# A pre-norm transformer block in float32: ScalarE's round-trip instructions queued behind the latest copy out of PSUM, and another spread of steps in the values' sweep

## The chip, the cores and the metric

The kernel runs on one core of one Trainium2 chip. A core has five engines that work side by side, each through its own queue in order: TensorE (PE in the profile; its weight loads are PEld), VectorE (DVE), ScalarE (ACT), GpSimd (POOL) and SyncE (SP, which here only issues DMAs). PE writes its products to PSUM, a small memory of its own; ACT and DVE copy from there to SBUF, the working memory. The metric is device time in microseconds (us) of the whole program, lower is better.

## The reference, cut to what matters

Input is one sequence of 2048 positions by 1024 features, everything float32. The feed-forward part has three weights of 2752 x 1024, which are put through a "round trip" before they are used: each block of 64 consecutive weights is divided by its largest absolute value, each quotient is replaced by the nearest of 16 fixed codes (NF4), and the block is multiplied by the same value again.

```python
def block(x):                                   # x: 2048 x 1024
    n = layernorm(x)
    q, k, v = (n @ w.T + b for w, b in ((wq, bq), (wk, bk), (wv, bv)))
    # 32 heads of 32; heads attend to heads within one position
    probs = softmax(einsum("shd,std->sht", q, k) / sqrt(32))
    x = x + einsum("sht,std->shd", probs, v)
    n = layernorm(x)
    w1, w2, w3 = (round_trip(w) for w in (W1, W2, W3))
    return x + (silu(n @ w1.T) * (n @ w2.T)) @ w3.T
```

## The kernel before, in words

**Products.** Large products are done with seven block products in place of eight (Strassen's scheme in Winograd's form). Operands are split in halves both ways, sums and differences of the quarters are made on DVE, and PE makes seven products 1 to 7. Some of them accumulate onto one another in PSUM: `z` takes products 1, 6, 5 and 3 in turn, and between two of them ACT has to copy the present state of `z` out (g0, u2, u4). So the next product into `z` waits for that copy. These are the copies that PE waits for.

**Stages.** First come three sweeps over eight pairs of 128-position tiles: queries, keys, values (`products`, line 348, called from the three loops at 531, 623 and 713). Within `products`, a function `fill(n)` is called behind each product; it puts other PE work between the products: transposes of the next tile (`transposes`, 467, or `keep_T`, 688), parts of the scores or of the context (`part`, 604; many small 32 x 32 products), and steps of the background. Then the feed-forward part ("the feed-forward stage" here) runs over 22 chunks of the hidden dimension: class `Unit` (877) makes the gate and up products and their Silu, and `down7` (980) the product with w3, whose results `give` (1000) copies to SBUF (`acc`, six buffers) and adds to x1 in DRAM by an accumulating DMA from POOL.

**The background: the round trip.** All 65 chunks of w1, w2 and w3 ("jobs") go through a generator, `background` (219), that is advanced a step at a time from the other code. A job is a load `wn` (SP); the largest values of the blocks (DVE, line 207); a division (16 ACT instructions of 64 columns, `scaled`, 192, line 195); 15 steps over 1024 columns, of which 12 are a pair, an ACT instruction that writes `sg` (line 242, two buffers) and a DVE instruction that merges it into `r` (line 243), and 3 are DVE alone (234, 236, 238); and the multiplication by the block's value, in the sweeps by 16 ACT instructions (line 195 again), in the feed-forward stage in turn by those or by one DVE instruction (line 254). Then `finish` (147) follows: PE transposes `r` in two halves of four (`ptw`, line 161), ACT copies each half out (`wop`, line 162), DVE makes the sums, SP stores the result, and a later DMA loads it as a weight.

**What sets the order.** PE's queue is in the order in which the program is traced (`manual_schedule` for PE, line 283): every transpose of `finish` has a fixed place between the products. The queues of ACT, DVE, POOL and SP are ordered when the kernel is built, by a planner that follows the dependences and its own idea of when each instruction can start; among instructions that it thinks ready, the one that was traced earlier goes first. An instruction of the background may so be put ahead of work that was traced long before it. In the sweeps the background advances by the numbers in `fill` (725 to 735 in the values' sweep, where `advance(2 if n == 6 else 1)` makes seven steps a pair of tiles) and by `advance(2)` after each pair; in the feed-forward stage by time: `spent` (794) advances 0.69 steps per microsecond of product. `pending` holds the jobs that wait for `finish`; `flush` (187) runs some of it, in the feed-forward stage mostly when the next job has reached its sixth step, or at once where a weight is needed (`until`, 264).

Of the kernel before, what the change touches and what calls it, by code (L numbers as in the profile page):

```python
# [2 lines left out]

# [1 line left out]

# [64 lines left out]
def preln_block_kernel(  # L70
# [38 lines left out]
    dqp = ctx.enter_context(tc.tile_pool(name="dq", bufs=2))  # L109
    fs = ctx.enter_context(tc.tile_pool(name="fs", bufs=2))  # L110
    hook = {"scale": "ACT"}

    def mean_var(pool, src, dst):
        st = pool.tile([P, 2, 6], FP, tag="st", name="st")
# [76 lines left out]

    def scaled(dst, src, by, nb):

        for n in range(nb):
            nc.scalar.mul(dst[:, ts(n, BLOCK)], src[:, ts(n, BLOCK)], by[:, n : n + 1])  # L195

    def width(kind, c):
        return KC * min(P, F - c * P) if kind == "3" else E
# [20 lines left out]
    def background():  # L219
        ready = load_w(*jobs[0])  # L220
        ahead = load_w(*jobs[1])
        am = absmax(*jobs[0], ready)
        yield
        for n, (kind, c) in enumerate(jobs):
            wn, wa = ready, am
            ready = ahead
            if n + 2 < len(jobs):
                ahead = load_w(*jobs[n + 2])
            w = width(kind, c)
            v = wn[:, :w]  # L230
            r = dqp.tile([P, E], FP, tag="r", name="r", bufs=2)[:, :w]
            for i, (side, edge, code) in enumerate(STEPS):
                if i == 0:
                    nc.vector.tensor_scalar(r, v, edge, code, ALU.is_lt, ALU.mult)
                elif side == "<":
                    nc.vector.scalar_tensor_tensor(r, v, edge, r, ALU.is_lt, ALU.max)
                elif side == ">":
                    nc.vector.scalar_tensor_tensor(r, v, edge, r, ALU.is_gt, ALU.subtract)
                else:
                    t = dqp.tile([P, E], FP, tag="sg", name="sg")[:, :w]  # L240
                    by = BIG if side == "+" else -BIG
                    nc.scalar.activation(t, v, AF.Copy, bias=-edge * by, scale=by)  # L242
                    nc.vector.scalar_tensor_tensor(r, t, code, r, ALU.min, ALU.max)  # L243
                step["n"] = i
                yield
                if i == 9 and n + 1 < len(jobs):
                    am = absmax(*jobs[n + 1], ready)
                    yield
            if hook["scale"] == "ACT" or n % 2:
                scaled(r, r, wa, w // BLOCK)  # L250
            else:
                r3 = r.rearrange("p (b e) -> p b e", e=BLOCK)
                f = wa[:, : w // BLOCK].unsqueeze(2).to_broadcast([P, w // BLOCK, BLOCK])
                nc.vector.tensor_tensor(r3, r3, f, ALU.mult)
            pending.append(finish(kind, c, r))
            yield
# [91 lines left out]
    def products(A, fill, used=lambda name: None, apart=None):  # L348

        def mul(dst, a, w, start, stop):
            mm4(dst, A[:, a], W[w], start, stop)
            used(w)

        def copied(nm, src):
            t = pair.tile([P, TB], FP, tag=nm, name=nm)
            nc.scalar.copy(t, src)  # L358
            return t

        z = ps_pj.tile([P, TB], FP, tag="z", name="z")
        mul(z, SA11, "B11", True, False)
        g0 = copied("g0", z)
        q = ps_pj.tile([P, TB], FP, tag="q", name="q")
        mul(q, S3, "T3", True, False)
        s7 = copied("s7", q)
        fill(7)
        mul(z, S2, "T2", False, False)
        u2 = copied("u2", z)
        fill(6)  # L370
        r = bank("r")
        mul(r, SA12, "B21", True, True)
        ce = pair.tile([P, E], FP, tag="C0", name="ce")
        co = pair.tile([P, E], FP, tag="C1", name="co")
        nc.vector.tensor_tensor(ce[:, 0:512], g0, r, ALU.add)
        fill(2)
        mul(z, S1, "T1", False, apart is not None)
        u4 = copied("u4", z)
        nc.vector.tensor_tensor(co[:, 512:], u4, s7, ALU.add)
        fill(5)  # L380
        if apart is None:
            mul(z, S4, "B22", False, True)
            nc.scalar.copy(ce[:, 512:], z)
        else:
            y = apart.tile([P, TB], FP, tag="y", name="y", bufs=1)
            mul(y, S4, "B22", True, True)
            nc.vector.tensor_tensor(ce[:, 512:], u4, y, ALU.add)
        fill(3)
        mul(q, SA22, "T4", False, True)
        nc.vector.tensor_tensor(co[:, 0:512], u2, q, ALU.add)  # L390
        fill(4)
        return ce, co
# [62 lines left out]
    class Inputs:  # L455
# [11 lines left out]
        def transposes(self, j):  # L467
            for half in range(2):
                pt = ps_t.tile([P, 4, P], FP, tag="pt", name="pt")
                for k in range(4):  # L470
                    nc.tensor.transpose(pt[:, k, :], self.xn[j][:, ts(4 * half + k, P)], ident)
                n = (SA11, SA12, SA21, SA22)[2 * j + half]
                a, v = (self.a21, self.v21) if n == SA21 else (self.A[:, n], self.V[:, n])
                nc.scalar.copy(a, pt)
                nc.scalar.copy(
                    v.rearrange("p k (c m) -> p k c m", c=4),
                    pt.rearrange("p k (m c) -> p k c m", c=4),
                )

        def finished(self):  # L480
# [207 lines left out]
    def keep_T(i, x1n):  # L688

        t = work.tile([P, 2, 4, P], FP, tag=f"xT{i % 2}", name="xT")  # L690
        for half in range(2):
            pt = bank("pt").rearrange("p (k t) -> p k t", t=P)
            for k in range(4):
                nc.tensor.transpose(pt[:, k, :], x1n[:, ts(4 * half + k, P)], ident)
            nc.scalar.copy(t[:, half], pt)
        cols = ts(i // 2 % 4, P)
        tbp = i // 8
        names = ("B11", "B21") if i % 2 == 0 else ("B12", "B22")
        for n in range(2):
            nc.sync.dma_start(xd[names[n], tbp][:, :, cols], t[:, n])  # L700
        if i % 2 == 0:
            even["t"] = t
            return
        b11, b21 = even["t"][:, 0], even["t"][:, 1]
        b12, b22 = t[:, 0], t[:, 1]
        u = {}
        for n in range(4):
            u[n + 1] = work.tile([P, 4, P], FP, tag="xU", name="xU", bufs=2)
            y, z = ((b12, b11), (b22, u.get(1)), (b22, b12), (b21, u.get(2)))[n]
            nc.vector.tensor_tensor(u[n + 1], y, z, ALU.subtract)  # L710
            nc.sync.dma_start(xd[f"T{n + 1}", tbp][:, :, cols], u[n + 1])

    for p in range(NP):
# [9 lines left out]
        def fill(n):  # L723
            if n in (7, 2, 5, 4) and (p, n) != (1, 7):
                part()
            advance(2 if n == 6 else 1)
            if n in (7, 4):
                flush(1)
            if n == 5 and i in x1n:
                keep_T(i, x1n.pop(i))  # L730
            if n == 3:
                if p == 0:
                    part()
                elif i + 1 in x1n:
                    keep_T(i + 1, x1n.pop(i + 1))
# [141 lines left out]
    class Unit:  # L877
# [13 lines left out]
        def first(self):  # L891
            self.z = ps_z.tile([P, TB], FP, tag="z", name="z")
            self.mul(1, self.z, True, False)
            self.g0 = hp.tile([P, TB], FP, tag="g0", name="g0", bufs=2)
            nc.scalar.copy(self.g0, self.z)

        def middle(self):
            q = self.q = ps_q.tile([P, TB], FP, tag="q", name="q")
            self.mul(7, q, True, False)
            self.mul(6, self.z, False, False)  # L900
            u2 = self.u2 = hp.tile([P, TB], FP, tag="u2", name="u2")
            nc.scalar.copy(u2, self.z)  # L902
            r = ps_r.tile([P, TB], FP, tag="r", name="rr")
            self.mul(2, r, True, True)
            nc.vector.tensor_tensor(self.g0, self.g0, r, ALU.add)
            nc.scalar.activation(self.g0, self.g0, AF.Silu)
            self.mul(5, self.z, False, False)
            u4 = hp.tile([P, TB], FP, tag="u4", name="u4")
            nc.scalar.copy(u4, self.z)  # L909
            self.h = [new_h(), new_h()]  # L910
            nc.vector.tensor_tensor(self.h[1], u4, q, ALU.add)

        def last(self, odd_done=None):
            self.mul(3, self.z, False, True)
            si = hp.tile([P, TB], FP, tag="si", name="si")
            nc.scalar.activation(si, self.z, AF.Silu)
            nc.vector.tensor_tensor(self.h[1], self.h[1], si, ALU.mult)
            if odd_done:
                odd_done(self.h[1])
# [60 lines left out]
    def down7(g, tbp, sides):  # L980
# [18 lines left out]

        def give(src, q, *places):  # L1000
            t = accp.tile([P, TB], FP, tag="acc", name="acc")
            nc.scalar.copy(t, src)  # L1002
            for j, n in places:
                nc.gpsimd.dma_start(x1d[8 * tbp + 2 * q + j][n], t, accum_op=ALU.add)  # L1004

# [161 lines left out]
```

## Time and profile before

| What | Value |
|---|---|
| Median of 3 runs (lowest, highest) | 2488.98 us (2482.63, 2490.45) |
| The profiled execution, its own time | 2493.95 us |
| Its span, first to last instruction | 2492.2 us, mean granted TensorE clock 0.990 |
| DVE busy | 1980.5 us, 79% |
| ACT busy | 1610.4 us, 65%, 3267 instructions |
| `sg` on ACT, line 242 | 780 x 1053 ns = 812.6 us |
| round trip's scalings on ACT, line 195 | 1032 x 340 ns and 608 x 341 ns |
| merge on DVE, line 243 | 780 x 1213 ns = 945.4 us |

Times in the trace are counted from the start of the span. The query sweep lies at about 0 to 260, keys to 560, values to 828, the feed-forward stage with the background to about 2260, and the rest is the feed-forward stage alone. A line of the timeline gives start, duration, engine, source line, operation, output and inputs, shapes and count; in brackets stands the engine's idle time just before and what ended it. One product of the schemes shows as eight PE instructions of 128 x 512 (four per product in `down7`): the trace holds two for each float32 product in the code. Successive ACT instructions overlap a little: `sg` of 1.05 us follow each other every 0.96 us, those of 64 columns every 0.24, copies of 512 columns every 0.48.

### The profile page before, as it was taken

How to read it: one execution, taken by the hardware profiler on the slowest of the kernel's cores; microseconds unless marked ns; L12 is line 12 of the kernel's file. 1: busy time of each engine (PE TensorE's matmuls, PEld its weight loads, DVE VectorE, ACT ScalarE, POOL GpSimd, SP SyncE). 2: the span in 40 equal slices, each digit the busy share in tenths (PEclk: the TensorE clock that was granted, in tenths of full speed). 3: DMA queues.
4: the chain of work that ended last, by engine and by line, in shares of the span. 5: the costliest groups of instructions: out<-in, count | busy, mean ns of one | idle time of the engine just before them, and what ended most of it. 6: DMA issues, size and time to landing. Idle time of an engine off the chain costs nothing.

```text
span 2492.2 us, 36722 instructions
## 1 busy us (share of the span) xinstructions
PE 2386.5 (96%) x14000; PEld 1116.4 (45%) x14000; DVE 1980.5 (79%) x2208; ACT 1610.4 (65%) x3267; POOL 279.1 (11%) x352
## 2 busy tenths in 40 slices
PE   7999999999899999999999999999999999999998
PEld 4444455545444444444444444444444444444433
DVE  8999788878988587889989798898988989871022
ACT  3566544444553378898888888889888788871200
POOL 1010000000000012030120301203012030120300
PEclk9999999999999999999999999999999999999999
DMA  8788643556669587394973949739487394872973
GB/s 309 300 295 341 233 162 120 223 199 222 211 229 320 195 288 168 118 190 155 320 170 119 196 143 303 176 127 189 157 290 174 135 195 159 279 164 72 189 271 143
DMA packets 177297, 513.90 MB, mean 206 GB/s; under 512 B 15904, under 2 KB 70176, under 8 KB 154720
## 3 DMA queue, kind: packets, MB, share of 16 engines
q1 hardware_dynamic: 136224, 438.08, 48.1%
q0 software_dynamic: 40320, 73.42, 18.3%
q8 instruction: 110, 1.80, 0.3%
q14 instruction: 67, 0.55, 0.1%
q10 hardware_dynamic: 576, 0.05, 0.0%
HBM read 283.69 MB, written 227.80 MB: 205 GB/s over the span
## 4 chain that ended last, share of the span: by engine, by line
issue 29%; ACT 12%; DVE 10%; PE 10%; DMA 7%; POOL 1%; DVEq 0%; SPq 0%; POOLq 0%; ACTq 0%
DVE r L243 7%; DMA x1d<-acc 6%; PE z L339 4%; ACT sg L242 4%; ACT wn L195 3%; ACT acc L1002 2%; ACT r L195 2%; PE q L339 2%; PE z L989 1%; POOL x1d L1004 1%; DMA out_dram<-acc 1%; PE rr L339 1%; PE y L989 1%; DMA acc<-x1d 1%; PE r L989 1%
## 5 line engine op out<-in xcount | busy, mean ns | idle before, releaser
L243 DVE SCALAR_TENSOR_TENSOR r<-sg,r 128x1024 f32<-128x1024 f32 x780 | 945.4, 1213 | 108.5 <-ACT sg L242 77.1
L242 ACT ACTIVATE sg<-wn 128x1024 f32<-128x1024 f32 x780 | 812.6, 1053 | 316.3 <-DVE r L243 300.8
L1004 POOL DMA_DIRECT2D x1d<-acc x280 | 243.7, 890 | 1288.1 <-ACT acc L1002 1145.4
L339 PE MATMUL z<-xB,w 128*128 128x512 f32 x720 | 324.3, 599 | 5.2 <-ACT u L909 3.4
L339 PE MATMUL z<-xT,w 128*128 128x512 f32 x656 | 296.5, 594 | 5.5 <-ACT u L902 5.4
L339 PE MATMUL q<-xT,w 128*128 128x512 f32 x656 | 291.6, 592 | 0.0
L195 ACT ACTIVATE wn<-wn,rc 128x64 f32<-128x64 f32 x1032 | 267.4, 340 | 27.2 <-DVE rc L215 27.2
L989 PE MATMUL z<-w,h 128*128 128x512 f32 x496 | 233.6, 598 | 10.0 <-ACT acc L1002 7.2
L339 PEld LDWEIGHTS z<-xB,w 128*128 128x128 f32 x720 | 134.9, 192 | 172.6 <-issue 152.8
L339 PEld LDWEIGHTS z<-xT,w 128*128 128x128 f32 x656 | 121.7, 190 | 154.3 <-issue 136.5
L339 PEld LDWEIGHTS q<-xT,w 128*128 128x128 f32 x656 | 123.3, 190 | 149.5 <-issue 145.9
L339 PE MATMUL z<-wT,A 128*128 128x512 f32 x384 | 179.6, 611 | 3.2 <-DVE wT L506 2.0
L339 PE MATMUL q<-wT,A 128*128 128x512 f32 x384 | 172.9, 593 | 2.0 <-DVE A L398 2.0
L339 PE MATMUL z<-wB,A 128*128 128x512 f32 x320 | 151.4, 618 | 13.7 <-ACT u L358 13.7
L195 ACT ACTIVATE r<-r,am 128x64 f32<-128x64 f32 x608 | 154.6, 341 | 13.8 <-DVE r L243 13.5
L989 PE MATMUL y<-w,h 128*128 128x512 f32 x320 | 150.4, 594 | 1.3 <-DVE h L968 1.1
L339 PE MATMUL rr<-xB,w 128*128 128x512 f32 x328 | 147.5, 592 | 0.0
L989 PEld LDWEIGHTS z<-w,h 128*128 128x128 f32 x496 | 92.2, 191 | 122.9 <-issue 95.8
L207 DVE TENSOR_REDUCE am<-wn 128x16 f32<-128x1024 f32 (+1 forms) x65 | 78.3, 1205 | 55.1 <-ACT r L195 49.3
L1002 ACT COPY acc<-z 128x512 f32<-128x512 f32 x160 | 93.1, 582 | 39.6 <-PE z L989 24.2
L339 PEld LDWEIGHTS q<-wT,A 128*128 128x128 f32 x384 | 72.0, 190 | 89.0 <-issue 83.7
L339 PEld LDWEIGHTS z<-wT,A 128*128 128x128 f32 x384 | 72.0, 194 | 84.4 <-issue 80.9
(132 smaller groups left out, 2587.9 us busy)
## 6 DMA issues: line engine op xcount, KB each, us to landing
x1d<-acc POOLq DMA_DIRECT2D x280, 256.0 KB, 6.1
wd<-wop SPq DMA_DIRECT2D x31, 2048.0 KB, 7.4
w<-wd SPq DMA_DIRECT2D x41, 1280.0 KB, 7.6
wn<-in_w_dram SPq DMA_DIRECT2D x63, 512.0 KB, 4.9
xT<-xdT SPq DMA_DIRECT2D x28, 1024.0 KB, 8.2
xB<-xdB SPq DMA_DIRECT2D x24, 1024.0 KB, 7.9
w<-wd SPq DMA_DIRECT2D x42, 512.0 KB, 4.8
w<-wd SPq DMA_DIRECT2D x10, 1536.0 KB, 7.5
```

The lines of the kernel that those rows point to most:

```text
L195: nc.scalar.mul(dst[:, ts(n, BLOCK)], src[:, ts(n, BLOCK)], by[:, n : n + 1])
L207: nc.vector.tensor_reduce(am[:, :nb], v.rearrange("p (b e) -> p b e", e=BLOCK), AX.X, ALU.max, apply_absolute_value=True,)
L242: nc.scalar.activation(t, v, AF.Copy, bias=-edge * by, scale=by)
L243: nc.vector.scalar_tensor_tensor(r, t, code, r, ALU.min, ALU.max)
L339: nc.tensor.matmul(dst, w[:, k, :], xop[:, k, :], start=start and k == 0, stop=stop and k == 3, skip_group_check=True,)
L989: nc.tensor.matmul(dst, side[n][:, ts(q, P)], w3T[g[2 * m]][:, W3[n]], start=start and m == 0, stop=stop and m == 1, skip_group_check=True,)
L1002: nc.scalar.copy(t, src)
L1004: nc.gpsimd.dma_start(x1d[8 * tbp + 2 * q + j][n], t, accum_op=ALU.add)
```

## The change

Three things are added or altered. `urgent(...)` marks a copy that PE waits for (it notes that instruction). `behind()` opens a block in which every ACT instruction that is traced gets an ordering edge to the copy noted last: in ACT's queue it has to come after it. No semaphore is added by this; it binds the planner. The block is opened around the round trip's ACT instructions, the scalings and `sg`. Marked as urgent are: the copies of `products` (358, 383), the second copy of each transposed bank (475), `keep_T`'s (695), the four of `Unit` (895, 902, 909, 916) and `give`'s (1002). The copies of `finish` (162) are neither marked nor placed behind. Third, in the values' sweep, the seven steps of a pair are spread otherwise: two behind product 7, two behind 6, one behind 5, two behind 3, none behind 2 and 4.

```diff
@@ -109,6 +109,15 @@
     hook = {"scale": "ACT"}
+    copy = {"last": None}
+
+    def urgent(ins):
+        copy["last"] = ins.ins
+        return ins
+
+    def behind():
+
+        return tc.issue_after(copy["last"]) if copy["last"] is not None else nullcontext()
@@ -191,8 +200,9 @@
     def scaled(dst, src, by, nb):
-        for n in range(nb):
-            nc.scalar.mul(dst[:, ts(n, BLOCK)], src[:, ts(n, BLOCK)], by[:, n : n + 1])
+        with behind():
+            for n in range(nb):
+                nc.scalar.mul(dst[:, ts(n, BLOCK)], src[:, ts(n, BLOCK)], by[:, n : n + 1])
@@ -239,7 +249,8 @@
                     by = BIG if side == "+" else -BIG
-                    nc.scalar.activation(t, v, AF.Copy, bias=-edge * by, scale=by)
+                    with behind():
+                        nc.scalar.activation(t, v, AF.Copy, bias=-edge * by, scale=by)
                     nc.vector.scalar_tensor_tensor(r, t, code, r, ALU.min, ALU.max)
@@ -355,7 +366,7 @@
         def copied(nm, src):
             t = pair.tile([P, TB], FP, tag=nm, name=nm)
-            nc.scalar.copy(t, src)
+            urgent(nc.scalar.copy(t, src))
             return t
@@ -380,7 +391,7 @@
-            nc.scalar.copy(ce[:, 512:], z)
+            urgent(nc.scalar.copy(ce[:, 512:], z))
@@ -472,9 +483,11 @@
                 nc.scalar.copy(a, pt)
-                nc.scalar.copy(
-                    v.rearrange("p k (c m) -> p k c m", c=4),
-                    pt.rearrange("p k (m c) -> p k c m", c=4),
+                urgent(
+                    nc.scalar.copy(
+                        v.rearrange("p k (c m) -> p k c m", c=4),
+                        pt.rearrange("p k (m c) -> p k c m", c=4),
+                    )
                 )
@@ -692,7 +705,7 @@
-            nc.scalar.copy(t[:, half], pt)
+            urgent(nc.scalar.copy(t[:, half], pt))
@@ -723,7 +736,7 @@
             if n in (7, 2, 5, 4) and (p, n) != (1, 7):
                 part()
-            advance(2 if n == 6 else 1)
+            advance({7: 2, 6: 2, 5: 1, 3: 2}.get(n, 0))
             if n in (7, 4):
                 flush(1)
@@ -892,28 +905,28 @@
-            nc.scalar.copy(self.g0, self.z)
+            urgent(nc.scalar.copy(self.g0, self.z))
...
-            nc.scalar.copy(u2, self.z)
+            urgent(nc.scalar.copy(u2, self.z))
...
-            nc.scalar.copy(u4, self.z)
+            urgent(nc.scalar.copy(u4, self.z))
...
-            nc.scalar.activation(si, self.z, AF.Silu)
+            urgent(nc.scalar.activation(si, self.z, AF.Silu))
@@ -999,7 +1012,7 @@
             t = accp.tile([P, TB], FP, tag="acc", name="acc")
-            nc.scalar.copy(t, src)
+            urgent(nc.scalar.copy(t, src))
```

## Prediction

> **What bounds the kernel now.** I read the page's busy shares and slices first, then PE's waits, then PE's timeline with its gaps, and ACT's timeline at those gaps.
>
> ```profile
> PE 2386.5 (96%) x14000; PEld 1116.4 (45%) x14000; DVE 1980.5 (79%) x2208; ACT 1610.4 (65%) x3267; POOL 279.1 (11%) x352
> ...
> PE   7999999999899999999999999999999999999998
> ...
> DVE  8999788878988587889989798898988989871022
> ACT  3566544444553378898888888889888788871200
> ```
>
> PE is the bound; DVE and ACT are eight to nine tenths busy until 2260, so they have little room to catch up. All gaps of PE in its timeline add to 96 us. Charged to ACT are 58.4: 13.5 in the query sweep, 2.1 at the start of the keys, 12.8 in the values, 30.0 in the feed-forward stage. PE's waits by line:
>
> ```profile
> PE z L339 <- ACT u L358: 14.9, 6, 4.4
> PE z L989 <- ACT acc L1002: 13.8, 12, 3.3
> PE pt L471 <- ACT V L475: 12.4, 4, 4.2
> PE ptw L161 <- ACT wop L162: 5.8, 8, 2.4
> ```
>
> The columns are total, times, longest. What such a gap is, PE first, then ACT, both at 620 to 634:
>
> ```profile
> 622.05 1.09 PE L694 MATMUL pt<-ident,x 128*128 128x128 f32 x8
> 627.45 5.40 PE L339 MATMUL z<-wB,A 128*128 128x512 f32 x8 [4.30 <-ACT u L358]
> ```
>
> ```profile
> 623.21 1.06 ACT L242 ACTIVATE sg<-wn 128x1024 f32<-128x1024 f32 x1 [6.05 <-DVE r L243]
> 624.53 1.06 ACT L242 ACTIVATE sg<-wn 128x1024 f32<-128x1024 f32 x1 [0.27 <-DVE r L243]
> 625.87 1.06 ACT L242 ACTIVATE sg<-wn 128x1024 f32<-128x1024 f32 x1 [0.27 <-DVE r L243]
> 626.83 0.57 ACT L358 COPY u<-z 128x512 f32<-128x512 f32 x1
> ```
>
> `z` was finished at 620.9, but its copy stood behind three `sg` that themselves waited 6.05 us for DVE. The product after the gap takes 5.40 us where the usual one takes 3.70: the granted clock is 0.69 from 627.4 to 632.9, so such a gap costs 1.7 us more. Of PE's gaps, those of 2.77 us and more are followed by this, those of 2.0 and 2.1 not.
>
> **What moves.** The two built queues, before and after, hold the same instructions; PE's is the same instruction for instruction. On ACT every round-trip instruction moves back or stays: by 50 to 110 us of before's time in the keys and values, by some 10 us in the feed-forward stage, if PE kept its times. SP's loads of `wn` move back with it; POOL's queue is unchanged. DVE executes its merges later in its queue. So the stalls above lose their cause, and the jobs lose their lead.
>
> **Gains.**
> - Queries: at 72.43 the gap is 4.21 because nine scalings and two `sg` stand before the copies. Without them the same order of copies leaves 1.32 (the row at 101.11): 2.9, and 1.7 of clock. At 210.77, 2.87 becomes 1.32: 1.55 and 1.7. At 101.11 the copies now alternate as at 128.33, where 0.34 is left: 1.0. At 264.17, 2.10 becomes about 0.7, the bare copy (0.57, and under 0.1 to hand over on each side, as from 627.40 to 627.45): 1.4. The 4.04 at 40.52 stays, its sixteen scalings stay in front. Sum 10.
> - Values: all 12.8 (4.30, 2.97, 4.36, 0.82, 0.38) and three times 1.7 of clock: 18. The new spread puts nothing behind product 2 and one step behind 5, so `u4` has at most two `sg` ahead, those traced behind product 6: 2.0 us, beside 4.7 us of PE work between (a product, a part of the context).
> - Feed-forward stage: of the 30.0, the `u` copies come in time where they were late (7.2) and so do five `acc` (7.3), with 3.1 of clock behind 1570.87. The rest stays: at 1246.66, for one, `acc` waited 1.24 us for its buffer's accumulating DMA. Sum 17.6.
>
> All gains: 46.
>
> **Costs: what is late next.** The transposes `ptw` stand at fixed places in PE's queue, and the lead covered them. At 1535, in before, PE and then ACT:
>
> ```profile
> 1534.87 0.60 PE L161 MATMUL ptw<-ident,r 128*128 128x128 f32 x4
> ```
>
> ```profile
> 1528.76 3.69 ACT L195 ACTIVATE r<-r,am 128x64 f32<-128x64 f32 x15 [0.17 <-DVE r L243]
> ...
> 1537.58 0.57 ACT L1002 COPY acc<-y 128x512 f32<-128x512 f32 x1
> 1538.05 0.59 ACT L162 COPY wop<-ptw 128x512 f32<-128x512 f32 x1
> ```
>
> The scalings of `r` ended 2.4 us before PE wanted them. In the new queue they stand behind that `acc<-y` and one more `sg`, and the product of this `y` is PE's last before `ptw`. So PE must wait, from the end of that product: 0.48 copy, 0.96 `sg`, eight scalings of 0.24 for the first half, about 0.2 of handovers: 3.5 (2.6 where no `sg` stands between), less 0.3, since the four transposes are worked off meanwhile. Going through all jobs with before's PE times:
> - Scaled by ACT, no product between: 5 jobs (1061, 1272, 1483, 1535, 1858), 3 x 2.3 + 2 x 3.2 = 13.3. One 1.72 product between: 2 jobs (1113, 1698), 1.5 + 0.6. One of 3.43 between: 5 jobs, nothing. Sum 15.4. Nothing is added here for copies queueing at ACT (about 4) or for DVE: from a job's last `sg` to the last scaling before took mostly 7.4 us where 6.3 is the bare sum. Taken: 20, ends 0 and 36.
> - Scaled by DVE: from the start of the last `sg` to the end of the multiplication the shortest in before is 3.9 us, all of it behind the copy ahead of that `sg`. Before's PE reaches `ptw` 0.3, 0.9, 2.2, 3.6 and 3.9 us behind that copy in five jobs (1724, 1562, 1622, 1781, 1405): 3.6 + 3.0 + 1.7 + 0.3 = 8.6; with DVE's merges queueing (slack in before was 0.1 to 2 us in the jobs from 1404 to 1562) taken as 14, ends 0 and 25.
> - Keys and values: the first `ptw` at 297.5 comes right behind the product whose copy precedes the scalings (2.6), the pair at 638.3 waits for all sixteen (1.4). 4.
> - The copies themselves: the background, now traced before the next copy and not ahead of its time, is first in line. The sixteen scalings of `wn` were cut up by copies (five or six at a time); now they come in one block, 3.9 us. 23 of the 252 `acc` copies before 2260 have over 4.1 us of round trip between them and the copy before, where it was 6. A block, an `sg` and two copies are 5.8 us; the next product into that `z` comes 3.4 us after the last. Worked out for each copy, PE is late at nine places by 0.3 to 5.4, 14 in all; `u` copies are late at ten by 0.3 to 2.3, 9. Taken 21, ends 0 and 44 (every lateness counted, also those that an earlier one swallows).
> - Clock: new gaps over 2.77 ahead of a first transpose are two or three: 4.
>
> Sum of costs 20 + 14 + 4 + 21 + 4 = 63. Net +17: 2494 + 17 = 2511 in this execution's terms. Its own time is 5 us above the median of the runs, so 2506 beside 2489.
>
> No row shows these new waits, so this sum is bounded: below by no wait at `ptw` and no late copy (costs 4 + 4, net -38), above by all upper ends (36 + 25 + 4 + 44 + 4 = 113, net +67); I take the middle, as the rows at 1404 to 1562, with slack near nothing, show that such waits exist.
>
> **A rule weighed.** In the rows here the clock fell behind gaps of 2.77 us and more, and the gap in front of the first transpose of a new wait is mostly below. The Trainium skill, TensorE: Matmul & The Clock Gate, section Why this matters for your kernels, warns of idle gaps over about 3 us; its Part 4 says that transposes don't count as busy in the same way. If that holds, a wait, four transposes worked off slowly and no product between make one long gap, some seven of the new waits would lose the clock, an estimate of 12 us in place of 4. No row here shows a transpose amid such waits.
>
> **Rivals.**
> - A, faster: the new waits are small, since a PE that waits once lets ACT and DVE catch up, and the lateness of one place swallows the next. With a quarter of the costs (16): net -30, 2459 beside the median. For it: the values' gaps are plain, and 58 us are charged to ACT. Against it: the new queue holds the scalings behind the copy, and PE has nothing else to do there.
> - B, cancelling: costs of 40 to 53, within 7.5 us (0.3%, about what a measurement of this kernel can tell from no change). The terms above are that close.
> - C, much slower: DVE becomes the bound in the feed-forward stage. It is 87% busy there, its merges wait for `sg` that wait for copies, and each `ptw` then waits for DVE. It decides where DVE is above 92%, as in 1450 to 1550 (92.67 of 100 us). With 1 us more at each of 54 jobs: net +50 to +70, 2540 and more.
> - D, it doesn't do what it says: some `sg` still stand before a late copy (the 4.04 at 40.52 does). That takes 5 to 10 off the gains and is in the range.
>
> **How the numbers follow.** Forecast (net +8 to +40) 0.42; C 0.13; B 0.17; A 0.28. Slower by over 0.3%: 0.55; within: 0.17; faster: 0.28. The range takes in A and most of C: 2455 to 2542. The forecast's own range is 2497 to 2529.
>
> **What would show it.** In the changed profile PE's waits on `u` of 358 in the values and the 5.40 products should be gone; if not, D. PE should wait at `ptw` for ACT's `r` (195's line) and DVE's, some 30 to 45 us where 0.4 was charged to DVE; if this is below 15, A. `acc` should keep over 10. DVE idle on `sg` should grow in 850 to 2250; if PE's gaps there exceed 90, C. I would be wrong by one mistake above all: taking PE's times as fixed, place by place.

## The result, and the profile after

The changed kernel takes 2523.67 us (2519.76 to 2530.7, 5 runs) beside 2488.98 (2482.63 to 2492.48, 5 runs): 1.0144 times as long, 95% interval 1.0127 to 1.0161. It is slower, as forecast, but by 34.7 us where 17 were forecast. The profiled execution took 2530.7 us (span 2528.9, mean granted clock 0.982 where it was 0.990). Both profiled executions lie above the median of their kernel's runs (after by 7 us, before by 5), so the difference of their spans, 36.7 us, may be taken apart place by place. Since runs of one kernel lie up to 11 us apart, a row of a stage table is good to some 5 us, an estimate.

From the page of the changed kernel:

```profile
PE 2403.9 (95%) x14000; PEld 1124.2 (44%) x14000; DVE 1983.8 (78%) x2208; ACT 1612.4 (64%) x3267; POOL 282.2 (11%) x352
```

The same instructions as before, and PE is busy 17 us longer: nearly all of that is half clock (15.6 by the table below), not work. PE's waits by line (total, times, longest):

```profile
PE ptw L170 <- DVE r L265: 17.6, 9, 2.9
PE ptw L170 <- ACT r L205: 13.9, 13, 3.1
PE z L1002 <- ACT acc L1015: 11.8, 10, 3.9
PE z L350 <- ACT u L922: 8.2, 5, 2.7
PE sc L430 <- DMA ql<-qD: 8.0, 1, 8.0
PE pt L482 <- ACT V L487: 6.7, 3, 4.0
```

`u` of the values is gone from this list and `V` of the queries is halved: the change does what it says. In their place stand the two waits at `ptw`, which were 0.4 us before, and one that the prediction did not have, `ql`. Since PE's queue is the same, the time at which PE starts the same product can be compared in the two timelines:

| Stage | after less before | PE idle | half clock |
|---|---|---|---|
| queries, from the first product on | -2.9 | -4.5 | +1.1 |
| seam to the keys, 271 to 307 | +12.8 | +9.6 | +3.2 |
| keys | -4.4 | -1.6 | -3.0 |
| values and the plain chunk, 560 to 835 | -14.4 | -13.0 | -1.9 |
| feed-forward stage to 2260 | +46.5 | +30.9 | +14.7 |
| rest | -0.5 | -1.8 | +1.5 |

"Half clock" is PE's busy time in the periods of half clock, halved: an estimate of what the lower clock cost. The seam is the passage from the queries to the keys.

**One wait at `ptw`.** PE, then ACT, both after:

```profile
1278.07 1.88 PE L1002 MATMUL z<-w,h 128*128 128x512 f32 x4
1281.30 1.28 PE L170 MATMUL ptw<-ident,r 128*128 128x128 f32 x3 [1.35 <-ACT r L205]
1282.73 0.47 PE L170 MATMUL ptw<-ident,r 128*128 128x128 f32 x1
1283.00 5.09 PE L350 MATMUL q<-xT,w 128*128 128x512 f32 x8
```

```profile
1279.99 0.59 ACT L1015 COPY acc<-z 128x512 f32<-128x512 f32 x1
1280.66 3.93 ACT L205 ACTIVATE r<-r,am 128x64 f32<-128x64 f32 x16
```

The transposes stand right behind the last product, the scalings right behind its copy, as the prediction had it. The gap is only 1.35 us, yet the next product takes 5.09. Two stretches of the same place, the columns being length, PE (busy), PEld, DVE, ACT, POOL, and then the granted clock:

```profile
1279.40:1282.80 3.40, 1.60 (x6) 0.48 (x4) 1.23 (x1) 3.31 (x12) 2.64 (x3) 0.97 1.04 193
1282.80:1286.20 3.40, 3.40 (x5) 1.54 (x6) 1.58 (x2) 3.40 (x11) 0.00 (x0) 0.53 1.08 212
```

PE was busy 1.60 of 3.40 us, most of it with transposes; the clock of the next 3.4 us is 0.53. The period of half clock itself begins at 1282.58; in the 3.41 us before it PE was busy for 1.76, a share of 0.52.

**The seam.** ACT, DVE, SP and PE after:

```profile
264.70 0.59 ACT L394 COPY ce<-z 128x512 f32<-128x512 f32 x1 [3.79 <-PE z L350]
265.18 2.00 ACT L253 ACTIVATE sg<-wn 128x1024 f32<-128x1024 f32 x2
```

```profile
266.27 1.22 DVE L254 SCALAR_TENSOR_TENSOR r<-sg,r 128x1024 f32<-128x1024 f32 x1 [4.64 <-ACT sg L253]
...
269.15 0.68 DVE L530 TENSOR_TENSOR cB<-cB,cB 128x512 f32<-128x512 f32 x1
```

```profile
250.91 0.33 SPq L541 DMA_DIRECT2D A<-opD  x1
269.87 1.52 SPq L534 DMA_DIRECT2D wtDv<-cB  x2
...
273.24 22.93 SPq L631 DMA_DIRECT2D ql<-qD  x4
```

```profile
282.95 1.77 PE L430 MATMUL sc<-kd,ql 32*32 32x32 f32 x128 [7.99 <-DMA ql<-qD]
284.66 5.99 PE L350 MATMUL z<-wT,A 128*128 128x512 f32 x8
```

Before, SP issued the same load at:

```profile
258.87 1.01 SPq L618 DMA_DIRECT2D ql<-qD  x2
```

To be read upwards: PE waits for `ql`; SP issued its load at 273 (258.87 before) because stores of the values' weights stood ahead of it for 19 us; these waited for sums on DVE; those stood behind a merge that waited 4.64 us for an `sg`; and that `sg` has its edge to a copy at 264.7.

### The profile page after: what moved, and what is told of

It reads as the page before. It is cut to its first block, busy times and chain, and to the rows that moved or that the text cites. A ratio compares the mean times of both kernels' runs of the same rounds, so it can differ in the third digit from the quotient of the medians.

```text
span 2528.9 us, 36662 instructions
## 1 busy us (share of the span) xinstructions
PE 2403.9 (95%) x14000; PEld 1124.2 (44%) x14000; DVE 1983.8 (78%) x2208; ACT 1612.4 (64%) x3267; POOL 282.2 (11%) x352
## 4 chain that ended last, share of the span: by engine, by line
PE 29%; DVE 14%; issue 12%; ACT 10%; DMA 3%; POOL 1%; DVEq 0%; SPq 0%; POOLq 0%; ACTq 0%
PE z L350 10%; DVE r L254 9%; PE z L1002 6%; PE q L350 4%; ACT wn L205 3%; ACT sg L253 3%; PE y L1002 3%; PE rr L350 2%; ACT r L205 2%; PE r L1002 1%; DMA x1d<-acc 1%; ACT acc L1015 1%; PE ptw L170 1%; POOL x1d L1017 1%; PE po L1073 1%
## 5 line engine op out<-in xcount | busy, mean ns | idle before, releaser
L205 ACT ACTIVATE wn<-wn,rc 128x64 f32<-128x64 f32 x1032 | 257.1, 340 | 6.5 <-DVE rc L225 6.5
L1002 PE MATMUL z<-w,h 128*128 128x512 f32 x496 | 239.3, 611 | 17.4 <-ACT acc L1015 10.7
L205 ACT ACTIVATE r<-r,am 128x64 f32<-128x64 f32 x608 | 149.5, 338 | 20.1 <-DVE r L254 20.1
L170 PE MATMUL ptw<-ident,r 128*128 128x128 f32 (+1 forms) x520 | 88.5, 281 | 37.8 <-DVE r L265 17.6
L369 ACT COPY u<-z 128x512 f32<-128x512 f32 x48 | 28.3, 590 | 140.7 <-PE z L350 140.3
```

Of the source, the lines that this page charges most:

```text
L170: nc.tensor.transpose(pt[:q, k, :], v[:, j * q : (j + 1) * q], ident)
L369: urgent(nc.scalar.copy(t, src))
L1002: nc.tensor.matmul(dst, side[n][:, ts(q, P)], w3T[g[2 * m]][:, W3[n]], start=start and m == 0, stop=stop and m == 1, skip_group_check=True,)
```

## The experiments

All were run beside the kernel before (2486.8 to 2487.6 us, 18 to 35 runs each). The table gives each median, the ratio with its interval (which is not the quotient of the two medians), and for the feed-forward stage the time against before's profile, PE's waits at `ptw` for `r`, and those for `acc` and `u`.

| Run | median us | ratio (95%) | stage | `ptw`←`r` | `acc`+`u` |
|---|---|---|---|---|---|
| before | 2487 | 1 | 0 | 0.4 | 24 |
| after | 2523.7 | 1.0144 (1.0127–1.0161) | +46.5 | 29.4 | 24.6 |
| e1 edges in the sweeps only | 2495.0 | 1.0029 (1.0018–1.0041) | -3.5 | 0.4 | 22 |
| e2 `ql` from POOL | 2524.5 | 1.0143 (1.0125–1.0161) | +50.9 | 30.5 | 24 |
| e3 later flush | 2533.0 | 1.0179 (1.0161–1.0197) | +50.5 | 32.4 | 27 |
| e4 no transposes right behind | 2489.7 | 1.0011 (1.0001–1.0021) | +7.7 | 0 | 39 |
| e5 edges in the values only | 2487.7 | 0.9999 (0.9986–1.0011) | -1.4 | 0.4 | 20 |
| e5b spread only | 2485.8 | 1.0002 (0.9991–1.0013) | -4.5 | 0.4 | 21 |
| e6 scalings free | 2492.6 | 1.0025 (1.0013–1.0037) | +15.4 | 11.2 | 21 |
| e7 edges from values to units | 2489.4 | 1.0014 (1.0005–1.0022) | +2.9 | 0.4 | 23 |
| e8 `sg` free | 2498.6 | 1.0039 (1.0025–1.0054) | +21.3 | 20.2 | 20 |
| e9 three mends | 2486.6 | 0.9993 (0.9982–1.0003) | +11.7 | 0 | 40 |
| e10 before, as e4 | 2485.7 | 0.9989 (0.9977–1.0001) | -5.7 | 0 | 13 |
| e11 `sg` edges, mends | 2490.4 | 1.0009 (0.9997–1.0021) | +13.4 | 0 | 39 |
| e12 waits filled | 2515.9 | 1.0117 (1.0104–1.013) | +37.4 | 15.9 | 18 |
| e13 e7 and later transposes | 2487.4 | 1.0001 (0.9993–1.001) | +2.6 | 0 | 17 |
| e14 thin handover | 2492.9 | 1.0028 (1.0017–1.0038) | +8.0 | 0 | 19 |
| e15 no edges in the queries | 2520.2 | 1.0135 (1.012–1.015) | +43.7 | 29.6 | 24 |
| e16 queries' waits filled | 2485.3 | 0.9996 (0.9986–1.0005) | -5.4 | 0 | 16 |
| e17 steps moved to the keys | 2497.7 | 1.0039 (1.0023–1.0055) | +1.0 | 0 | 13 |

**Which stage pays.** e1 drops the edges where the feed-forward stage begins:

```diff
-        return tc.issue_after(copy["last"]) if copy["last"] is not None else nullcontext()
+        return tc.issue_after(copy["last"]) if copy["last"] is not None and hook["scale"] == "ACT" else nullcontext()
```

> The changed kernel with the edges left out in the feed-forward stage, kept in the three sweeps. Place by place the changed trace stands against the one before at -2.9 us in the queries, +12.8 at the seam to the keys, -4.4 in the keys, -14.4 in the values, +46.5 in the feed-forward stage. Theory: the +46.5 belong to the edges of that stage alone (31 us of PE idle, 15 of clock). Then -9 is left, 2480 beside 2489, PE's idle time in that stage goes back to 34 to 38 us and PE's waits at ptw for r there are under 2 us. Rival: part of it is inherited from the sweeps, whose jobs reach the stage in another phase; then at least 15 us stay, 2495 or more.

Measured: the stage's +46.5 became -3.5 and its waits at `ptw` for `r` 0.4, so the loss belongs to that stage's edges; nothing is inherited. But the time fell by 29, not 44, to the rival's 2495, though not for the rival's reason: the values kept only 4.1 of their 14.4 by 835 (0.6 by 845), and after's profile lies above its median, this one below.

e5 has a flag in the condition, set before the values' loop and cleared behind it:

```diff
+    copy["on"] = True
     for p in range(NP):          # the values' loop
...
     hook["scale"] = "DVE"
+    copy["on"] = False
```

> Edges in the values' sweep alone, with the new spread of steps there; the queries, the keys and the feed-forward stage without edges. Theory: the values' gain (14.4 us) needs nothing from the other sweeps, and the seam's +12.8 comes with the queries' edges: 2474, PE's waits for u in the values 0, no wait for ql. Rival: without the edges in the sweeps ahead the steps come into the values in another phase and the gain shrinks to half, 2482; or the feed-forward stage pays for the later steps, 2485 or more.

Measured: no wait for `ql`, none for `u` in the values, 12 us gained there by 770, and a total within 0.1% of before. The edges end at about 770, behind the values' loop, and the gain is given back by 840. PE in e5:

```profile
819.61 1.94 PE L707 MATMUL pt<-ident,x 128*128 128x128 f32 x8 [4.74 <-DVE x L345]
833.43 3.70 PE L350 MATMUL z<-xT,w 128*128 128x512 f32 x8 [3.14 <-ACT g L910]
```

PE now waits for other work of DVE and ACT. That DVE is making up the delayed steps there is a reading that fits; it isn't shown.

**The seam.** e2 issues the loads of `ql` from POOL, e15 sets the flag before the keys' loop and never clears it:

```diff
-            nc.sync.dma_start(t, src[2 * p + j])
+            (nc.gpsimd if tag == "ql" else nc.sync).dma_start(t, src[2 * p + j])
```

> The changed kernel, with the loads of ql issued from POOL's queue instead of SP's. Theory: PE's wait of 8.0 us for ql at 283 (and 2.3 of clock behind it) is a matter of SP's queue alone: the loads stand behind four stores of the values' weights whose sums DVE makes late. Then both go: 2513 beside 2524, and the first scores start right behind the product ahead of them. Rival: the loads are late for another cause (their buffers, the transfer itself); then 4 us or more of the wait stay and the time is 2519 or more.

> The changed kernel without the queries' edges (keys, values and feed-forward stage as changed). Theory: the seam's +12.8 comes of the queries' edges (a merge that waits for a late sg holds the sums of the values' weights, and those hold SP's queue and with it ql); without them the seam is as before, and the queries lose their -3: 2514 beside 2524. Rival: as with ql issued from POOL, the wait goes and the total stays within 3 us of 2524: it is given back later.

Measured: in both the wait for `ql` is gone, the seam is +6.1 and +4.1 where it was +12.8. So the place is as explained. The total did not follow in e2 (2524.5) and followed by 3.5 of the 10 in e15. Half clock in the feed-forward stage costs 4.5 us more in e2's profile than in after's, and single runs of after lie up to 11 us apart; whether the seam's 7 to 9 us are given back or drown in that stays open.

**Lead.** (The lead is how long a job is ready before PE asks for it.) e3 lets `flush` run from the next job's eighth step; e4 takes away the places right behind the scalings.

```diff
-        if finish and step["n"] in range(5, 15):
+        if finish and step["n"] in range(8, 15):
```

> The changed kernel, with the transposes ptw of the feed-forward stage placed from the next job's eighth step on instead of its fifth. Three steps are 4.3 us of products. Theory: the 31 us that PE waits at ptw there are lead that the edges took away, so a later place gives them back: waits at ptw 5 to 8 us, the clock loss of the stage 15 to about 6, some 5 us lost to weights that are stored later: 2492 to 2502. Rival (DVE and ACT are the bound of that stage): the waits only move, those at ptw stay over 20 us in sum or as much turns up at u, acc and w; 2515 or more.

```diff
             pending.append(finish(kind, c, r))
+            step["n"] = 15 if n + 1 < len(jobs) else 14
             yield
```

> The changed kernel, with one place moved: where the transposes of a job fell right behind its scalings (23 of the 54 jobs of the feed-forward stage, since the step count of the finished job still stands when the next product asks) they now come with the next job's fifth step, 7 to 10 us of products later, the second half 3.4 later. All but two of PE's waits at ptw in the changed profile lie at these 23 places; the run with the later flush left these places where they were and so did not test the lead. Theory (lead): these waits (31 us idle) and most of the clock lost there (15) go: 2482 to 2490. Rival (the chain of sg and merge is the bound of the stage): the waits come back elsewhere, 2510 or more.

Measured: e3 changed nothing for the better, since the waiting transposes did not move. The count still says 14 when a job is finished, so where a product asks just then, the first half is placed at once. That holds for 23 of the stage's 54 jobs, and the 17 places of the stage where PE waits at `ptw` for `r` are all among them; two more are in the sweeps. e4 moves the transposes, and 34 of the 36 us (2523.7 beside 2487.6) are gone; the stage's half clock costs 9.5 us in place of 19.4. The same edit on the kernel before, e10 below, changes the time by 0.1%, so the later place is no gain of that size in itself. That is the cause of most of the loss: at these places a job has no lead but the one the planner gives it, and the edges take it. The rival is right in part: with no wait at `ptw`, the copies come late instead, 39 us of waits for `acc` and `u` where there were 25. PE's waits in e4:

```profile
PE z L1003 <- ACT acc L1016: 18.5, 15, 3.8
PE z L351 <- ACT u L923: 12.6, 8, 3.0
```

**Which instructions.** e6 opens `behind()` in `scaled` only in the sweeps, e8 around `sg` only in the sweeps:

```diff
-        with behind():
+        with behind() if hook["scale"] == "ACT" else nullcontext():
```

> The changed kernel, with the scalings of the feed-forward stage without edges (sg keep theirs). Theory: PE's waits at ptw for ACT's r (12.9 us) come from the scalings being placed behind the copy; they fall under 4, those for DVE's r (17.6) stay: 2506 to 2510. Rival: the scalings are late because the last merge is late, which the edges of sg cause; then 9 or more of the 12.9 stay and the time is 2518 or more.

> The changed kernel, with sg of the feed-forward stage without edges, the scalings there keep theirs: the mirror of the run with free scalings, which came to 2493 and not to the 2506 to 2510 expected, because the waits for DVE's r fell as well (17.6 to 4.9). An edit of the scalings of r alone gives the same queues as the changed kernel, so that result belongs to the sixteen scalings of wn. Theory: in one block of 3.9 us behind a copy they make the last sg of a job late; with sg free the block stays, so PE still waits 20 us or more at ptw: 2510 to 2520. Rival: the edges of sg are needed for the loss; with sg free the waits at ptw fall under 10: 2500 or less.

Measured: either half of the edges alone costs far less than both: 5 and 11 us above before, where both cost 36. Both expectations were wrong in size; e8's time is its rival's, its 20 us of waits at `ptw` are its theory's. DVE's waits from 850 to 2250 tell what the scalings of `wn` do, first after, then e6:

```profile
DVE r L254 <- ACT sg L253: 60.0, 118, 2.7
DVE am L217 <- ACT r L205: 55.3, 21, 4.0
DVE r L244 <- ACT wn L205: 54.3, 28, 3.8
```

```profile
DVE r L244 <- ACT wn L205: 18.6, 17, 2.8
```

Line 244 is the first step of a job. After, it waits 54 us for scaled weights, a wait that before's list doesn't have; with free scalings 19 are left. In e8 it is 58, yet the time is 25 us better, so this wait alone isn't the loss either. That the block of scalings and the late `sg` add up in front of transposes that have no slack fits both runs; it isn't shown. Nor has a run the scalings of `wn` alone free: e6 frees those of `r` with them.

**The values.** e5b has the new spread and no edges; e7 clears the flag only ahead of the first `Unit`; e13 is e7 with e4's edit; e14 drops the three steps of the plain chunk; e17 has `advance(3)` per pair in the keys and `advance(1)` in the values.

```diff
-            advance(2 if n == 6 else 1)
+            advance({7: 2, 6: 2, 5: 1, 3: 2}.get(n, 0))
```

> The kernel before with the new spread of the values' steps alone, no edges anywhere. With edges in the values alone and this spread PE's waits for u were gone there (12.8 before). Theory: edges and spread each take part; the spread alone leaves 5 to 9 us of these waits, 2483 beside 2487. Rival 1: the spread alone does it, waits for u under 2. Rival 2: it does nothing, 12 or more.

> Edges from the start of the values' sweep to the first chunk that runs by seven products (so in the plain chunk at 780 to 840 too), new spread, no edges before or after. With the edges ending before the plain chunk the values had gained 12 us by 770 and given 12 back by 840 (waits of DVE's x, of cx, of the first copy g). Theory: the give-back comes from the planner's putting the delayed steps ahead of the copies where the edges end; with edges there it stays small: 2478 beside 2487. Rival: the delayed work has to be done anyway and is paid in the first units: 2485 or more.

> Edges from the values' sweep to the first units, new spread, and the later transposes of the feed-forward stage; no edges elsewhere. The two parts alone gave 2489 and 2486 beside 2487. Theory: the values' 7 to 12 us and the stage's 3 to 5 add up, 2480. Rival: the steps delayed in the values are paid in the first units (a first copy g late by 4.6 us there), 2486 or more.

> As the run before it, without the three steps of the background in the plain chunk at 780 to 840, so that the steps delayed in the values have room there; the later steps come three sooner in the count, at the same pace. Theory: DVE's backlog at the handover (waits of the transposes for x, of cx, of z for g: some 12 us) is what gives the values' gain back; with three steps fewer (about 7 us of DVE and ACT) half of it goes: 4 to 6 us faster than the run before it. Rival: the steps are missing later (weights late, waits for w of 3 us and more): no gain or slower.

> As the run with edges in the values and the later transposes (2487), with eight steps of the background moved from the pairs of the values' sweep to those of the keys. Theory: what gives the values' gain back at 770 to 840 is that DVE and ACT come there without the lead that the planner built up before; eight steps fewer (some 18 us of DVE) in the values leave room, and the keys have it (DVE 81% busy there): the waits of 5 to 6 us for x and g fall under 2 each, 2479 to 2482. Rival: the steps are only late elsewhere, in the keys or at the first transposes: 2486 or more.

Measured: the spread alone leaves 12.6 us of waits for `u`, so the edges took them away; whether they need the new spread for it is open, since no run has the edges with the old one. None of e7, e13, e14, e17 keeps the gain: 2487 to 2498. e14 loses 7 us from 2063 to 2172, still in the feed-forward stage (among them waits of 2.9 for `wop` and 1.4 for `u`), e17 its gain in the values outright (waits of 3.2 at `ptw` and 5.6 for `x` there). The delayed steps were paid at each of the places tried; the theory of a backlog that only needs spreading has fallen.

**The clock.** e12 adds work in front of the transposes at the places right behind the scalings; e16 does the like at three places of the queries, in the bank of `y`, on e10.

```diff
+            if half == 0 and step["n"] == 14 and hook["scale"] == "DVE":
+                for k in range(4):
+                    nc.tensor.matmul(pt[:, k, :], ident, ident, start=True, stop=True)
```

> The changed kernel, with four added matmuls of 128 columns in front of the transposes at the 24 places right behind a job's scalings (their result is overwritten by the transposes), so that PE works 0.9 us of its wait away. The queues of ACT and DVE differ from the changed kernel's in a few rows only. Theory (clock): in the changed profile a stretch of half clock follows a 3.4 us stretch in which PE was busy under about 0.45, or up to 0.62 where most of it was transposes; five of the nine such stretches of the feed-forward stage (1282, 1528, 1532, 1562, 1754) lie at these waits. With 0.9 us of work in each (0.26 of a stretch) they go: half clock in the stage 44 us before, 25 to 30 then, and the time falls by 5 to 8, to 2517, although PE has more to do. Rival: the clock follows the wait itself, whatever PE does beside it, or the work only adds: half clock stays over 40, 2524 to 2532.

> The kernel before with the later transposes (2486 beside 2487 alone) and twelve added matmuls of 128 columns, 2.6 us, in a bank of their own at three places of the queries where PE waits 2.8 to 4.6 us for the copy V (41, 73 and 212 in the run with the later transposes; two of them are followed by 3.4 to 6.8 us of half clock). Nothing reads what they write. Theory (clock, as in the run with the filled waits): the waits shrink by 2.6 each and the half clock behind them goes, 3 to 5 us: 2481 to 2483. Rival: the bank of the added matmuls is waited for in its turn, or the clock is no better: 2486 or more.

Measured: e12 has the expected time (2515.9) and the expected half clock (27 us of periods, after 44), but not for the reason given. Of the five stretches named, those at 1528, 1532 and 1754 are gone; the two others are still there:

```profile
1268.40 1.05 PE L170 MATMUL ptw<-ident 128*128 128x128 f32 x8
1271.49 1.91 PE L173 MATMUL ptw<-ident,r 128*128 128x128 f32 x4 [2.04 <-ACT r L208]
1273.19 5.08 PE L353 MATMUL q<-xT,w 128*128 128x512 f32 x8
```

PE worked 1.05 us there, but the scalings came later too: 2.04 us of idle time are left where there were 1.35, and the next product is as slow as it was. So the added work did not shorten this wait. Two new stretches came (1713, 1877), and the largest gains lie elsewhere: 5.8 us at 1248, where a copy `acc` that was 3.87 late no longer is, presumably since a few rows of ACT's queue are ordered otherwise. So e12 tells nothing sure of the clock, and that its time came out as expected is luck. e16 shortened the waits for `V` from 12.8 to 5.6 and gained nothing: the added work took what it filled.

**Versions put together.** e9 has e6's, e4's and e2's edits; e11 the same with the scalings free in the sweeps too; e10 is before with e4's edit.

> The changed kernel with three mends: scalings free in the feed-forward stage, no transposes right behind a job's scalings, loads of ql from POOL's queue. From the stages of the runs with one mend each: queries -3, seam +6, keys -4, values -12, feed-forward stage -3 (its +15 less the 14 of waits at ptw and some 5 of clock), in sum -16 against the profile of before: 2472 to 2478 beside 2487. Rival: with the waits at ptw gone the copies acc and u come late by as much as in the run with the later transposes (39 us of waits for them instead of 25): 2485 or more.

> As the run with three mends, but the scalings are free in the sweeps too, so that only sg have edges. Theory: in the queries the scalings cost the wait of 4.0 at 41 either way and gain 4 to 5 at 72 to 211 by their edges, in the values the edges of the scalings matter little: 3 to 6 us slower than the run with three mends. Rival: the block of sixteen scalings of wn is what makes sg late in the sweeps as in the feed-forward stage, at the seam above all (sums of the values' weights behind a merge that waits 4.6 us for sg); then it is 3 us or more faster.

> The kernel before with the later transposes alone, as a control for the runs that have them. There PE waits 5.7 us at ptw for the copy wop and 0.4 for r. Theory: there is no lead to give back, so nothing is gained but part of the 5.7: 2483 to 2488. Rival: later weights cost as much or more, 2490 or more.

Measured: e9 and e11 came out as e9's rival says, with 40 and 39 us of waits for `acc` and `u`. With edges in the feed-forward stage their sum with the waits at `ptw` for `r` was 32 to 59 us in every run, without edges there 13 to 25. No version is surely faster than before; the nearest is e10, 0.9989 with an interval that reaches 1.0001.

## Why the prediction was right in direction and short by half

The time lies inside the forecast's own range, 2497 to 2529, but the change is twice the sum. By its own terms, place by place in the two profiles:

| Step | predicted | measured |
|---|---|---|
| queries: four gaps | -10 | -9.1 there, +6.2 at places not foreseen |
| seam, `ptw` at 297 | +2.6 | +2.5 |
| seam, `ql` | not priced | +10.3 |
| keys | 0 | -4.4 |
| values | -18 + 1.4 | -14.4 |
| stage: `u` and `acc`, gains and lateness | -14.5 + 21 | +0.4 |
| stage: waits at `ptw` for `r` | 20 + 14 | 29.4 (11.8 ACT, 17.6 DVE) |
| stage: clock | -3.1 + 4 | +14.7 |
| stage: `wop`, `w` | 0 | -4.9, +3.9 |

The stage's rows leave some 3 us of its 46.5; the list of waits leaves out gaps under 0.15 us, such as those between the transposes of one wait.

**Right.** The values, the four gaps of the queries (at 264 a gap of 0.68 is left, "about 0.7"; at 101 only 0.3 of the 1.0 came), the two terms at `ptw` and the 2.6 at the seam are there in size and place. All twelve jobs with a price at `ptw` wait after: the seven scaled by ACT 11.3 us (15.4 worked out), the five by DVE 9.9 (8.6 worked out); five others wait 8.2. That the copies gain nothing in the feed-forward stage holds too, though as 0 and not as 6.5. Slack near nothing at 1404 to 1562 was the right row to go by: the same jobs wait after.

**The step that failed: "new gaps over 2.77 ahead of a first transpose are two or three: 4".** Half clock cost 19.4 us in the stage, where before's was 4.6: 14.7 more, where the prediction had 4 less 3.1. It looked for new half clock ahead of transposes alone, and gave the late copies, which it priced, none. In the changed profile four periods in the stage lie at waits at `ptw` (1282, 1528, 1562, 1754) and cost 8.1 us; six lie at waits for `u`, `acc` and `w` (846, 924, 1057, 1252, 2054, 2191) and cost 11.3. Two of these six:

```profile
1056.75 5.40 PE L350 MATMUL z<-xB,w 128*128 128x512 f32 x8 [2.28 <-ACT u L922]
1251.36 5.40 PE L1002 MATMUL z<-w,h 128*128 128x512 f32 x8 [3.87 <-ACT acc L1015]
```

The waits for `u` and `acc` have the sum that they had before, but they are 18 where they were 27, and five are over 2.2 us where one was.

The prediction also took the length of one gap as the condition, from gaps of 2.77 and more. Rows of before speak against that:

```profile
509.44 0.34 PE L419 MATMUL sc<-kd,ql 32*32 32x32 f32 x6 [2.09 <-issue]
...
510.62 6.04 PE L339 MATMUL z<-wT,A 128*128 128x512 f32 x8
...
2458.69 1.98 PE L1060 MATMUL po<-w,h 128*128 128x512 f32 x4 [2.76 <-DVE h L917]
```

Half clock begins at 508.7, in the gap of 2.09; behind that of 2.76 the granted clock stays at 1.00. The profiles show another condition. The periods of half clock are 3.41, 6.83 or 10.24 us long and start on a grid of 3.413 (a period that the end of the kernel cuts short is left out). If PE's timeline is cut on that grid in the twenty profiles of this case (stretches already at half clock, the first 20 us and the last 40 left out), what follows a stretch hangs on PE's busy share in it:

| PE busy in the stretch | large products | over 0.2 transposes | over 0.2 products of 32 x 32 |
|---|---|---|---|
| under 0.40 | 140 of 140 | 16 of 16 | 8 of 8 |
| 0.40 to 0.55 | 10 of 88 | 18 of 36 | 20 of 20 |
| 0.55 to 0.70 | 0 of over 180 | 19 of 75 | 7 of 34 |
| 0.70 and more | 0 of over 11,500 | 4 of over 450 | 0 of over 1,100 |

The second and third columns hold the stretches with over 0.2 of their length in transposes or in products of 32 x 32, the first all others; the cells count those that half clock followed. So a gap of 2.1 us may cost the clock or not, as it falls on the grid; two short gaps add up; and transposes count for less than their time, which fits the 1.35 us that were enough at 1281. The Trainium skill, TensorE: Matmul & The Clock Gate, section What's actually happening, has a free-running window of 3413 ns, and the traces agree with it; the "over about 3 us" of idle time that the prediction weighed is too long a limit by these counts. The estimate of 12 us by the rule on transposes, weighed and not taken there, was nearer in number, but the transposes' places cost 8.1. The counts show that the clock goes with this share; no run changed the share alone at one place, and that it would have given 14.7 beforehand is not shown, since the grid lies anew in every run (the clock first changes at 13.78 us before, at 12.82 after).

**The second: what moves with an instruction.** "SP's loads of `wn` move back with it" was followed; that a merge on DVE waits in front of other sums, and these in front of SP's stores and the next stage's loads, was not. That is +10.3 at the seam in the profile. The queries' further +3.9 at 168 is a new wait at `ptw` of 1.0 us, its slow transposes and 1.7 of clock, the same mechanism that was priced at 297.

**Terms that offset them.** The copies were set at +6.5 and came to +0.4: a PE that waits at `ptw` lets ACT catch up, as rival A said. e4, without these waits, has 14 us more of waits for the copies, and e10, the same edit without edges, 11 less than before, so they come of the edges. The keys' -4.4 is mostly 3.0 of half clock in before's profile; six of the seven kernels that have no edges there and before's steps have -3.5 to -4.8 as well (e16 has 0.0). So that the measured time came into the forecast's range is in part luck: the clock (13.8 over), `ql` (10.3) and the queries (7.1) stand against the copies (6.1 under), the waits at `ptw` (4.6) and the keys (4.4).

**The rivals.** A fell: the waits at `ptw` are 29.4, above its 15. C fell: DVE is busy 85% of the time from 850 to 2250, not over 92, its wait on `sg` fell from 76.8 to 60.0 where it was to grow (the new wait is that of line 244), and PE's gaps there are 63 us, not over 90. B fell by the time, which is 34.7 us off and not within 7.5. D fell, with one correction: the waits for `u` in the values are gone, but of the sweep's slow products two are still there (5.29 us at 630.60, 4.71 at 764.94), behind other waits. The mistake named beforehand, PE's times taken as fixed place by place, cost some 6 us in the copies; the clock cost more.

## What to carry to other kernels

Before an instruction is bound behind another, count who stands directly behind its result: here the transposes of 23 jobs had no slack of their own, and moving these alone took back 34 of 36 us. An in-order queue passes lateness on: follow the late instruction through each engine that waits for it, the DMA queue included, to the next stage. And set a price on short waits of PE by how much work is left in the stretch around them, not by the length of one gap.

## What the runs showed of the hardware that was not expected

The sharpness of the clock's condition: of 140 stretches with large products and a busy share under 0.40 all were followed by half clock, of over 11,700 at 0.55 or more none. The spread of one kernel's runs goes with the granted clock: after's five runs lie from 2519.76 us at a granted clock of 0.987 to 2530.7 at 0.982.
